# One buffer of exponentials instead of two, two group loads moved into segment 2, and eight groups corrected without VectorE

## The chip, the cores and the metric

The kernel runs on one core of a Trainium2 chip. Its engines work side by side: TensorE (PE) multiplies matrices, ScalarE (ACT) applies functions and copies, VectorE (DVE) does element-wise work, GpSimd (POOL) issues the gathers and scatters that take row numbers, and SyncE (SP) issues the plain transfers. Sixteen transfer engines, shared by all issuers, move the data between HBM and the on-chip memory. The metric is the device time of one execution in microseconds (us); the span of a profile is the time from the first to the last instruction of the program in one profiled execution.

## What is computed

The input is a table of 16384 rows of 256 floats and a segment number from 0 to 7 for each row. The numbers are not sorted. `searchsorted` over them gives a start for each segment, and a row takes part in its segment's attention if its distance from that start fits into a padded table of 3072 places (a negative distance counts from the end). Cut to what matters:

```python
q, k, v = feat @ Wq, feat @ Wk, feat @ Wv
starts = jnp.searchsorted(bids, jnp.arange(B))
pos = jnp.arange(N) - starts[bids]
qp, kp, vp = (zeros(B, LMAX, ...).at[bids, pos].set(x) for x in (q, k, v))
scores = where(mask, einsum('bld,bmd->blm', qp, kp), NEG)
rp = einsum('blm,bmd->bld', softmax(scores), vp)
t = rp[bids, pos] @ Wt
tn = (t - t.mean(0)) / sqrt(t.var(0) + EPS) * gamma + beta
return feat + relu(tn)
```

A row that lies outside its segment's table reads the row at the table's edge, so most of the 16384 results are `feat` plus one of at most sixteen edge rows, and only some 4700 rows have a result of their own.

## The kernel before

The function `fast_path` records all instructions of the five engines in one order, and a small recording layer (`Program.op`, L587, and `settle`, L625) works out from the memory that each reads and writes which semaphores it waits for. Nothing reorders an engine's instructions: the order of the calls is the order on each engine. A transfer issued by SyncE waits, and everything behind it on SyncE waits with it.

**The attention** runs over the eight segments (the loop at L1743, index `e`, and `u` for steps within a segment). A segment has up to six tiles of 128 rows. GpSimd gathers a segment's rows into `xs` two segments ahead (`list_half`, L1202, issued at step 0); one segment ahead they are transposed (`xt_main`, step 0), multiplied into queries and keys (`project`, L1252, steps 1 and 3) and values (`values`, L1272). `scores` (L1285) forms the products of keys and queries; ScalarE writes their exponentials, for the first four query tiles into `pa` and for the last two into `pb`. `attend` (L1318) multiplies the exponentials with the values, `attended` (L1328) divides and writes the result to `tk`, and SyncE stores it to the table `t_rows` in HBM, four tiles after step 3 and two after step 5. Of `q`, `k`, `vs` and `pa` there are two buffers each, which segments take in turn (`e % 2`). The exponentials of segment e+1 are made at steps 3 and 4 of segment e, after the `attend` calls for tiles 0 to 3.

**The statistics.** `acc` collects sums and squares of the results; the squares of the last tiles lie in `sq`, four slots behind `tk`. After segment 7 TensorE forms `sums` from them (L1888 to L1898), and a short chain on VectorE and ScalarE makes the scale, the shift and the table `y3` of corrected edge rows.

**The tail** (L1903 to L2038). The 16384 rows are cut into 16 groups of 1024 rows (1 MB). For each group a load `group_in` (L1723) brings `feat` into a buffer; a unit of two tiles is corrected by adding a product of the one-hot table `hot` with `y3`; the group is stored. There are four units in a group and two ways to correct one. In the first, VectorE adds the product, in PSUM, to the buffer (L2002). In the second, TensorE first multiplies the buffer with the identity into the same PSUM bank, adds the product there, and ScalarE copies the bank back (L1991, L1998). `by_act` (L1987) says which unit goes which way. Groups are worked in pairs (index `c`), and PSUM banks 0 to 5 are taken in turn.

There are `NF` = 12 buffers `f0` to `f11` for the 16 groups. Most of them lie over memory that the attention has finished with, so that a load waits until that memory is free. `free_at` (L983) lists their places: three rooms of their own (groups 0 to 2), the lists (group 3), the region from `q0` to `pa0` (4 and 5), that of `w4`, `wvt`, `xT` and `vs0` (6 and 7), that of `q1`, `k1` and `pa1` (8 and 9), and that of `sq`, `pb` and `vs1` (10 and 11). Groups 12 to 15 take the buffers of groups 0 to 3 after these are stored.

Between the pairs, VectorE normalises the attention's own rows (`rows`, L1968), and GpSimd writes them over the stored groups, 128 rows at a time (`put`, L892). It may only do so after every group that holds rows of that segment has been stored: SyncE waits for a store to land and adds one to the semaphore `done` (`finish`, L1978), and GpSimd waits for a count worked out from the segment numbers. With this input the counts are 3 for segment 0, 5 for segments 1 and 2, 7 for segments 3 to 5 and 11 for segments 6 and 7. At most two stores stand behind the one that SyncE waits for (L2011).

Of the kernel before, what the change touches and what calls it, by code (L numbers as in the profile page):

```python
# [9 lines left out]
F32 = mybir.dt.float32  # L10
# [4 lines left out]
AF = mybir.ActivationFunctionType  # L15
# [5 lines left out]
P = 128  # L21
NB = 8
# [6 lines left out]
FT = 6  # L29
# [873 lines left out]
def fast_path(nc, feat, bids, wq, wk, wv, wt, gamma, beta, out, bad):  # L903
# [5 lines left out]
    GT = 8  # L909
# [19 lines left out]
    def new(name, shape, dtype=F32):  # L929
        nonlocal end  # L930
        size = mybir.dt.size(dtype)
        for d in shape[1:]:
            size *= d
        plan.append((name, shape, dtype, end))
        h = at(name, shape, dtype, end)
        end += size + -size % 32
        return h
# [8 lines left out]
    def addr(h):  # L946
        return pg.where[h.name][1]
# [4 lines left out]
    def tiles_of(e):  # L952
        return FT if e else 4

    rooms = [new(f"room{i}", [P, GT, D]) for i in range(3)]
    xs = new("xs", [P, TS, D])
    hot = new("hot", [P, NG // 2, GT, P], F8)
    SQ = 4
    tk = new("tk", [P, TS + SQ, D])
    sq = [tk[:, TS + i, :] for i in range(SQ)]  # L960
    pa, vs, q, k = [None] * 2, [None] * 2, [None] * 2, [None] * 2
    at_end = addr(tk) + TS * D * 4
    pb = new("pb", [P, FT, QB])
    vs[1] = new("vs1", [P, FT, D + 1])
    at_scores = end
    q[1], k[1] = new("q1", [P, FT * P]), new("k1", [P, 2, P])
    pa[1] = new("pa1", [P, FT, QA])
    at_values = end
    junk = [new("junk0", [P, P]), new("junk1", [P, P])]
    w4, wvt = new("w4", [P, DH, P]), new("wvt", [P, DH, D])  # L970
    xT = new("xT", [P, DH, FT * P])
    vs[0] = new("vs0", [P, FT, D + 1])
    at_before = end
    q[0], k[0] = new("q0", [P, FT * P]), new("k0", [P, 2, P])
    pa[0] = new("pa0", [P, FT, QA])
    at_lists = end
    lm, dl = new("lm", [P, NL, J], BF16), new("dl", [P, 2, J + 2], BF16)
    ge = new("ge", [P, 2, FT * P], BF16)
# [2 lines left out]
    crow, cown, cidx = new("crow", [32, 1], I32), new("cown", [32, 1]), new("cidx", [32, 1], I32)  # L981
    cdiag = new("cdiag", [32, 2 * NB])
    free_at = [addr(x) for x in rooms] + [at_lists]  # L983
    for x in (at_before, at_values, at_scores, at_end):
        free_at += [x, x + 8192]
    NF = len(free_at)
    fb = [at(f"f{i}", [P, GT, D], F32, x) for i, x in enumerate(free_at)]

# [1 line left out]
    ones_n = new("ones_n", [P, P])  # L990
    acc = new("acc", [P, 2, D])
    by_reads = new("by_reads", [P, 3, P])
    ecat = new("ecat", [P, 2, D])
    xl, tl = new("xl", [P, LT, D]), new("tl", [P, LT, D])
    eb = [new("eb0", [P, GT * P], BF16), new("eb1", [P, GT * P], BF16)]
# [256 lines left out]
    def project(e, c):  # L1252

        b = nb()
        lo, n = c * QA, (QA if c == 0 else QB)
        for t in (None,) if c == 0 else (4, 5):
            at0, w = (0, QA) if t is None else ((t - 4) * P, P)
            with present(e, t or 0):
                for h in range(DH):
                    pg.mm(  # L1260
                        b[:, at0 : at0 + w], w4[:, h, :], xT[:, h, lo + at0 : lo + at0 + w],
                        start=(h == 0), stop=(h == DH - 1),
                    )
        qe, ke = q[e % 2], k[e % 2]
        with present(e, 4 * c):
            pg.act(qe[0:96, lo : lo + n], b[0:96, 0:n], AF.Identity, bias=cqk[0:96, :])
            pg.act(qe[96:P, lo : lo + n], b[0:32, 0:n], AF.Identity, bias=cqk[0:32, :])
            for t in range(n // P):
                g = 32 * t
                pg.copy("DVE", ke[g : g + 32, c, :], b[96:P, t * P : (t + 1) * P])  # L1270
# [12 lines left out]
            pg.copy("ACT", vs[e % 2][:, 2 * c : 2 * c + 2, 0:D], b[:].rearrange("p (t d) -> p t d", t=2))  # L1283

    def scores(e, c, tiles):  # L1285
        qe, ke = q[e % 2], k[e % 2]

        def bank_of(t, lo, w):
            at0 = lo + (QB if t >= 4 and c == 1 else 0)
            return ps_s[t % 4][:, at0 : at0 + w]  # L1290

        def product(t, lo, w):
            g = slice(32 * (t % 4), 32 * (t % 4) + 32)
            pg.mm(bank_of(t, lo, w), ke[g, t // 4, :], qe[g, c * QA + lo : c * QA + lo + w])

        if c == 0:
            for t in tiles:
                with present(e, t):
                    product(t, 0, QA)
            for t in tiles:  # L1300
                with present(e, t):
                    m = e * FT + t
                    pg.act(pa[e % 2][:, t, :], bank_of(t, 0, QA), AF.Exp, bias=mask[:, m : m + 1])
            return
        with pg.given(e, 0):
            for t in range(5):
                product(t, 0, P)
        with pg.given(e, 1):
            for t in range(5):
                product(t, P, P)  # L1310
            product(5, 0, QB)
        for k_, parts in ((0, [(t, 0, P) for t in range(5)]), (1, [(t, P, P) for t in range(5)] + [(5, 0, QB)])):
            with pg.given(e, k_):
                for t, lo, w in parts:
                    m = e * FT + t
                    pg.act(pb[:, t, lo : lo + w], bank_of(t, lo, w), AF.Exp, bias=mask[:, m : m + 1])

    def attend(e, u):  # L1318
        po = ps_o[u % 2]
        src, w = (pa[e % 2], u) if u < 4 else (pb, u - 4)  # L1320
        for t in (0, 1, 2, 4, 5, 3) if e else range(4):
            with present(e, max(t, u)):
                pg.mm(
                    po[:, 0 : D + 1], src[:, t, w * P : (w + 1) * P], vs[e % 2][:, t, :],
                    start=(t == 0), stop=(t == 3),
                )
# [396 lines left out]
    def group_in(i, after=()):  # L1723
        pg.dma("SP", fb[i % NF][:], feat3[ORDER[i]], after)

    def repeated(t):
        pg.act(rsq[:], tl[:, t, :], AF.Square)
        pg.tt(acc[:, 0, :], acc[:, 0, :], tl[:, t, :], ALU.add)
        pg.tt(acc[:, 1, :], acc[:, 1, :], rsq[:], ALU.add)

    lag, ready = [], []
    steps = {0: (1, 2, 3, 4, 5), 1: (0, 1, 3), 2: (1, 2, 3, 5)}
    def third_list():
# [9 lines left out]
    for e in range(NB - 1):  # L1743
# [10 lines left out]
        for u in range(FT):  # L1754
# [43 lines left out]
            if u == 0:  # L1798
                if ahead < NB:
                    second()  # L1800
                if e == NB - 2:
                    for t in range(LT):
                        pg.gather(tl[:, t, :], t_rows[0 : (NB - 2) * FW, :], ridl[:, t : t + 1], (NB - 2) * FW)
                    group_in(3)
                if e:
                    xt_main(n, 0)
                    xt_main(n, 1)
# [20 lines left out]
                    ready.append(lag.pop(0))  # L1828
            if e == 0 and u in (1, 5):
                pg.copy("ACT", spot[:], ones[:, 0:1])  # L1830
            if e == NB - 3 and u in (1, 2, 4):
                group_in(u // 2 if u > 1 else 0)
            if e == NB - 2 and u == 4:
                pg.gather(ecat[:, 0, :], t_rows[0:EDGE, :], eidx[:], EDGE)
                group_in(4)
                group_in(5)
            if e == NB - 2 and u >= 3:
                repeated(u - 3)
            if e == 4 and u == 3:
# [66 lines left out]
    units = 0  # L1906
    pg.set("POOL", y3[:], 0.0)
    group_in(10)
    for t in range(LT):
        pg.gather(tl[:, t, :], t_rows, ridl[:, t : t + 1], NB * FW)  # L1910

# [70 lines left out]
    for c in range(NG // 2):  # L1982
        for r in range(2):
            i = 2 * c + r
            for x in range(0, GT, 2):
                early = (i, x) in first_units
                by_act = x >= (2 if 4 <= c < 7 else 4) if c else x in (2, 4) and early  # L1987
                pf = bank[units % 6]
                units += 1
                if by_act and not early:  # L1990
                    pg.mm(pf[:], ident[:], unit(i, x), start=True, stop=False)  # L1991
                for u in range(2):
                    pg.mm(
                        pf[:, u * D : (u + 1) * D], hot[:, c, x + u, :], y3[:, r, :],
                        start=not (by_act or early), stop=True,
                    )
                if by_act:
                    pg.copy("ACT", unit(i, x), pf[:])  # L1998
                elif early:
                    pg.copy("DVE", unit(i, x), pf[:])  # L2000
                else:
                    pg.tt(unit(i, x), unit(i, x), pf[:], ALU.add)  # L2002
            f = fb[i % NF]
            stores.append(
                pg.op("SP", lambda e, i=i, f=f: e.dma_start(out3[ORDER[i]], f[:]), [f[:]], [], dma=True)
            )
            if i == 2:
                group_in(NF - 1)
            if i >= 4 and i - 4 + NF < NG:
                group_in(i - 4 + NF)  # L2010
            while counted < i - 1 or counted < min(i, 3):  # L2011
                finish(stores[counted])
                counted += 1
        for e in {1: (0,), 2: (1,), 3: (2,), 4: (3, 4), 5: (5, 6), 6: (7,)}.get(c, ()):
            rows(e)
        if c == 6:
            normal([(ExitStack, tl[:, a:b, :], xl[:, a:b, :], b - a) for a, b in ((0, 2), (2, LT))])
        if c == 7:
            pg.ts(good[:], rdens[:], LIM, ALU.is_lt)
            pg.stt(good[:], rdens[:], 1.0 / LIM, good[:], ALU.is_gt, ALU.mult, accum=odd[:])  # L2020
            pg.ts(odd[:], odd[:], -1.0, ALU.mult, float(TT), ALU.add)
            pg.red(cnt_f[:, 0:1], over[:])
# [78 lines left out]
```

## Time and profile before

| | us |
|---|---|
| median of 3 runs | 284.02 |
| the 3 runs | 282.41, 284.02, 286.15 |
| time of the profiled execution | 284.55 |
| its span | 282.2 |
| PE busy | 242.6 |
| DVE busy | 195.5 |
| ACT busy | 140.0 |
| POOL busy | 106.2 |

Busy times are of the whole span, in which the attention and the tail have different limits, so they are read together with the stretches that the prediction quotes. A row of the table of stretches names the stretch, its length, then for each engine its busy time and the number of its instructions, then the granted clock of TensorE, the share of the sixteen transfer engines that was busy, and what they moved in GB/s. In a row of the timeline stand the start, the duration, the engine (with a q where its sequencer issues a transfer), the line, the operation, what it writes `<-` what it reads, how many such instructions were merged, and in brackets the idle time before and what ended it. A merged row's duration runs from the first start to the last end. The line of most instructions is that of a helper (L808 is `mm`, L827 `tt`, L880 `dma`), so the tile names tell them apart; `f` is a group's buffer, `out<-f` its store, `out<-tk` a write of single rows.

### The profile page before, as it was taken

Reading aid. Unit: us, or ns where it says so; the run is one execution under the profiler, and the core shown is the slowest. Engines: PE = TensorE matmul, PEld = TensorE weight load, DVE = VectorE, ACT = ScalarE, POOL = GpSimd, SP = SyncE. Lnnn points to the kernel's source line nnn. Section 1 sums busy time; section 2 is a strip of 40 time slices with the busy share of each in tenths; the row PEclk is TensorE's granted clock in tenths of the full one; section 3 lists DMA queues with packets and bytes.
Section 4 is the critical chain, followed back from the end, with each engine's and each line's share of the span. In section 5 each row is a group of like instructions: output and inputs, shape, how many; then the busy total and the mean of one; then the engine's idle time right before and its main releaser. Section 6 shows DMA issues by size and latency. Waiting matters only on the chain.

```text
span 282.2 us, 4370 instructions
## 1 busy us (share of the span) xinstructions
PE 242.6 (86%) x1219; PEld 168.7 (60%) x1219; DVE 195.5 (69%) x631; ACT 140.0 (50%) x304; POOL 106.2 (38%) x141
## 2 busy tenths in 40 slices
PE   1789979999999999999999999989998898195540
PEld 0656757667778777877787787667554444042210
DVE  8766887768878553465438618955499999999920
ACT  6246553792794764666546644586233344032210
POOL 4517174407104500256317001210030527577774
PEclk9999999999999999999999999999999999779975
DMA  3202799523122330221238485199989999999994
GB/s 101 58 7 77 243 336 363 177 90 97 30 74 85 110 103 8 95 82 54 89 85 251 147 263 180 35 345 394 352 340 361 378 415 412 404 408 388 396 368 171
DMA packets 24643, 59.06 MB, mean 209 GB/s; under 512 B 4355, under 2 KB 17005, under 8 KB 20517
## 3 DMA queue, kind: packets, MB, share of 16 engines
q1 hardware_dynamic: 19013, 47.74, 46.6%
q0 software_dynamic: 4784, 10.17, 10.8%
q10 hardware_dynamic: 816, 0.79, 0.8%
q8 instruction: 14, 0.23, 0.3%
q14 instruction: 16, 0.13, 0.1%
HBM read 26.93 MB, written 28.54 MB: 197 GB/s over the span
## 4 chain that ended last, share of the span: by engine, by line
PE 63%; DVE 21%; ACT 5%; issue 5%; POOL 2%; DVEq 1%; POOLq 0%; ACTq 0%
PE ps L808 60%; DVE ps L827 4%; PE ps L813 3%; DVE f L827 3%; DVE tk L827 3%; DVE tk L849 2%; POOL out L895 2%; ACT tk L818 2%; ACT pa L818 2%; DVE k L824 1%; DVEq L773 1%; ACT vs L823 1%; DVE sel L838 1%; DVE acc L827 0%; DVE w L827 0%
## 5 line engine op out<-in xcount | busy, mean ns | idle before, releaser
L885 POOL DMA_INDIRECT xs<-in_r_feat,idx x46 | 47.2, 1026 | 90.5 <-DVE idx L827 48.8
L808 PE MATMUL ps<-vs,pa 128*128 128x257 f32 x312 | 74.4, 386 | 1.8 <-ACT tk L818 1.5
L808 PEld LDWEIGHTS ps<-vs,pa 128*128 128x128 f32 x312 | 57.0, 190 | 12.7 <-ACT tk L818 2.8
L808 PE MATMUL ps<-f,ident 128*128 128x512 f32 x80 | 44.1, 645 | 15.8 <-DVE f L827 15.8
L895 POOL DMA_INDIRECT out<-tk,idx x39 | 38.4, 985 | 25.9 <-DVE tk L827 8.6
L823 ACT COPY f<-ps 128x512 f32<-128x512 f32 x37 | 21.5, 586 | 46.0 <-PE ps L808 46.0
L818 ACT ACTIVATE tk<-ps,rdens 128x256 f32<-128x256 f32 x48 | 22.6, 481 | 40.8 <-DVE rdens L862 40.6
L1363 DVE SCALAR_TENSOR_TENSOR acc<-tk,reads_r,acc 128x512 f32<-128x512 f32 x43 | 32.2, 748 | 9.9 <-ACT tk L818 9.3
L808 PE MATMUL ps<-wvt,xT 128*128 128x256 f32 x156 | 36.5, 383 | 0.0
L808 PEld LDWEIGHTS ps<-wvt,xT 128*128 128x128 f32 x156 | 29.1, 190 | 8.0 <-issue 2.8
L818 ACT ACTIVATE pa<-ps,mask 128x512 f32<-128x512 f32 x39 | 23.9, 689 | 7.8 <-PE ps L808 7.8
L808 PEld LDWEIGHTS ps<-y,hot 128*128 128x128 fp8e4 x128 | 12.7, 100 | 23.9 <-issue 21.8
L808 PEld LDWEIGHTS ps<-f,ident 128*128 128x128 f32 x80 | 13.3, 202 | 20.6 <-DVE f L827 11.5
L862 DVE RECIPROCAL rdens<-ps 128x1 f32<-128x1 f32 x44 | 7.4, 168 | 21.9 <-PE ps L808 21.7
L808 PE MATMUL ps<-y,hot 128*128 128x256 bf16 x128 | 20.4, 278 | 0.4 <-DVE y L827 0.4
L824 DVE COPY k<-ps 32x128 f32<-32x128 f32 x40 | 11.8, 294 | 11.7 <-PE ps L808 11.0
L808 PE MATMUL ps<-xT,w 128*128 128x512 f32 (+1 forms) x60 | 19.3, 453 | 0.5 <-ACT xT L818 0.3
L808 PE MATMUL ps<-vs,pb 128*128 128x257 f32 x82 | 19.6, 387 | 0.0
L808 PE MATMUL ps<-q,k 32*128 32x512 f32 (+2 forms) x154 | 18.9, 478 | 0.0
L808 PEld LDWEIGHTS ps<-vs,pb 128*128 128x128 f32 x82 | 15.1, 189 | 5.7 <-issue 2.3
L885 POOL DMA_INDIRECT tl<-t_rows,places x6 | 6.0, 999 | 31.5 <-DMA t_rows<-tk 20.2
L834 DVE TENSOR_SCALAR_CACHE_REDUCE junk<-ps,rcol 128x128 f32<-128x128 f32 x49 | 14.6, 346 | 4.4 <-PE ps L808 4.4
(259 smaller groups left out, 330.1 us busy)
## 6 DMA issues: line engine op xcount, KB each, us to landing
f<-in_r_feat SPq DMA_DIRECT2D x16, 1024.0 KB, 10.2
out<-f SPq DMA_DIRECT2D x16, 1024.0 KB, 10.1
xs<-zt SPq DMA_DIRECT2D x6, 768.0 KB, 7.4
t_rows<-tk SPq DMA_DIRECT2D x8, 512.0 KB, 3.3
eb<-edge_of SPq DMA_DIRECT2D x16, 128.0 KB, 3.2
t_rows<-tk SPq DMA_DIRECT2D x6, 256.0 KB, 2.4
xs<-in_r_feat,idx POOLq DMA_INDIRECT x46, 3.0
out<-tk,idx POOLq DMA_INDIRECT x39, 6.2
```

What stands on the lines that cost most here:

```text
L808: "PE", lambda e: e.matmul(out, lhsT, rhs, start=start, stop=stop, skip_group_check=True),
L813: return self.op("PE", lambda e: e.transpose(out, in_, ident), [in_, ident], [out])
L818: "ACT", lambda e: e.activation(out, in_, func, bias=bias, scale=scale), [in_, *more], [out]
L823: return self.op("ACT", lambda e: e.copy(out, in_), [in_], [out])
L824: return self.op(eng, lambda e: e.tensor_copy(out, in_), [in_], [out])
L827: return self.op(eng, lambda e: e.tensor_tensor(out, a, b, op), [a, b], [out])
L834: lambda e: e.tensor_scalar(out, a, s1, s2, op0, op1, accum_out=accum, **({"saturate": False} if out.dtype == F8 else {}))
L849: else e.scalar_tensor_tensor(out, a, s, b, op0, op1),
L862: return self.op("DVE", lambda e: e.reciprocal(out, in_), [in_], [out])
L885: lambda e: e.indirect_dma_start(out=out, out_offset=None, in_=table, in_offset=bass.IndirectOffsetOnAxis(ap=ind, axis=0), bounds_check=n ...
L895: lambda e: e.indirect_dma_start(out=table, out_offset=bass.IndirectOffsetOnAxis(ap=ind, axis=0), in_=src, in_offset=None, bounds_check=n ...
L1363: lambda e: e.scalar_tensor_tensor(acc[:], two, one, acc[:], ALU.mult, ALU.add),
```

## The change

The second buffers of `q` and `pa` go, and their room is given to two more rooms for groups, so that there are still twelve buffers. `k0` moves into the region of `w4`, and the two junk tiles of the list search (which are written and never read) into the room of `by_reads`, which is filled only in segment 7. The loads of groups 0 and 1 are issued in segment 2, at steps 2 and 4, those of groups 2 to 4 in segment 5 at the places where groups 0 to 2 were, that of group 5 where that of group 3 was. The places of groups 10 and 11 are swapped, and group 11's load goes out behind that of group 10. `finish` is called for stores 0 to 2 only when store 3 has been issued. Of the last eight groups all units go by TensorE and ScalarE.

```diff
-    rooms = [new(f"room{i}", [P, GT, D]) for i in range(3)]
+    rooms = [new(f"room{i}", [P, GT, D]) for i in range(5)]
...
-    q[1], k[1] = new("q1", [P, FT * P]), new("k1", [P, 2, P])
-    pa[1] = new("pa1", [P, FT, QA])
+    q, k[1] = new("q", [P, FT * P]), new("k1", [P, 2, P])
+    pa = new("pa", [P, FT, QA])
     at_values = end
-    junk = [new("junk0", [P, P]), new("junk1", [P, P])]
+    k[0] = new("k0", [P, 2, P])
...
-    at_before = end
-    q[0], k[0] = new("q0", [P, FT * P]), new("k0", [P, 2, P])
-    pa[0] = new("pa0", [P, FT, QA])
...
-    for x in (at_before, at_values, at_scores, at_end):
+    for x in (at_values, at_scores):
         free_at += [x, x + 8192]
+    free_at += [at_end + 8192, at_end]
...
+    junk = [at(f"junk{i}", [P, P], F32, addr(by_reads) + i * P * 4) for i in range(2)]
...
-                    pg.act(pa[e % 2][:, t, :], bank_of(t, 0, QA), AF.Exp, bias=mask[:, m : m + 1])
+                    pg.act(pa[:, t, :], bank_of(t, 0, QA), AF.Exp, bias=mask[:, m : m + 1])
...
+    EARLY = ((2, 2), (2, 4), (NB - 3, 1), (NB - 3, 2), (NB - 3, 4))
...
-                    group_in(3)
+                    group_in(5)
...
-            if e == NB - 3 and u in (1, 2, 4):
-                group_in(u // 2 if u > 1 else 0)
+            if (e, u) in EARLY:
+                group_in(EARLY.index((e, u)))
             if e == NB - 2 and u == 4:
                 pg.gather(ecat[:, 0, :], t_rows[0:EDGE, :], eidx[:], EDGE)
-                group_in(4)
-                group_in(5)
...
     group_in(10)
+    group_in(11)
...
-                by_act = x >= (2 if 4 <= c < 7 else 4) if c else x in (2, 4) and early
+                by_act = x >= (0 if c >= 4 else 4) if c else x in (2, 4) and early
...
-            if i == 2:
-                group_in(NF - 1)
             if i >= 4 and i - 4 + NF < NG:
                 group_in(i - 4 + NF)
-            while counted < i - 1 or counted < min(i, 3):
+            while i > 2 and counted < max(3, i - 1):
```

How SyncE's queue stands in segment 2, before (`tk` is the attention's result, `row_i` the table of row numbers, `at_h` that of the edge rows; a number behind a name is the program's):

```order
L880 DMA t_rows<-tk_54 128x2x256
L880 DMA t_rows<-tk_54 128x4x256
L880 DMA row_of<-row_i_182 128x128
L880 DMA t_rows<-tk_54 128x2x256
L880 DMA edge_of<-at_h_178 128x128
```

The same place after:

```order
L880 DMA t_rows<-tk_56 128x2x256
L880 DMA f0_78<-in_r_feat 128x2048
L880 DMA t_rows<-tk_56 128x4x256
L880 DMA f1_79<-in_r_feat 128x2048
L880 DMA row_of<-row_i_182 128x128
L880 DMA t_rows<-tk_56 128x2x256
L880 DMA edge_of<-at_h_178 128x128
```

The loads of groups 0 and 1 now stand ahead of the stores of segment 2's rows and of the table of row numbers. SyncE's queue from segment 6 to the first stores, before:

```order
L880 DMA f5_85<-in_r_feat 128x2048
L880 DMA f6_86<-in_r_feat 128x2048
L880 DMA f7_87<-in_r_feat 128x2048
L880 DMA t_rows<-tk_54 128x4x256
L880 DMA f8_88<-in_r_feat 128x2048
L880 DMA f9_89<-in_r_feat 128x2048
L880 DMA t_rows<-tk_54 128x2x256
L880 DMA f10_90<-in_r_feat 128x2048
L2005 DMA out_0<-f0_80 128x2048
L2005 DMA out_0<-f1_81 128x2048
L2005 DMA out_0<-f2_82 128x2048
L880 DMA f11_91<-in_r_feat 128x2048
```

And after:

```order
L880 DMA t_rows<-tk_56 128x4x256
L880 DMA f6_84<-in_r_feat 128x2048
L880 DMA f7_85<-in_r_feat 128x2048
L880 DMA t_rows<-tk_56 128x4x256
L880 DMA f8_86<-in_r_feat 128x2048
L880 DMA f9_87<-in_r_feat 128x2048
L880 DMA t_rows<-tk_56 128x2x256
L880 DMA f10_88<-in_r_feat 128x2048
L880 DMA f11_89<-in_r_feat 128x2048
L2004 DMA out_0<-f0_78 128x2048
L2004 DMA out_0<-f1_79 128x2048
L2004 DMA out_0<-f2_80 128x2048
```

The load of group 6 now follows segment 6's store of its first four tiles directly, and the load of group 11 has moved from behind the third store to ahead of the first. On TensorE, where group 8 begins (`ident` is the identity, `hot` the one-hot table, `ps` a PSUM bank), before:

```order
L808 MATMUL ps2<-y3_108,hot_53 128x256 x2
L808 MATMUL ps3<-f8_88,ident_92 128x512
L808 MATMUL ps3<-y3_108,hot_53 128x256 x2
L808 MATMUL ps4<-f8_88,ident_92 128x512
L808 MATMUL ps4<-y3_108,hot_53 128x256 x2
```

And after:

```order
L808 MATMUL ps2<-f8_86,ident_90 128x512
L808 MATMUL ps2<-y3_108,hot_55 128x256 x2
L808 MATMUL ps3<-f8_86,ident_90 128x512
L808 MATMUL ps3<-y3_108,hot_55 128x256 x2
L808 MATMUL ps4<-f8_86,ident_90 128x512
L808 MATMUL ps4<-y3_108,hot_55 128x256 x2
```

The first unit of group 8, which VectorE added to its buffer before, now has a product with the identity as well.

More of the change, by code (lines that the diff above doesn't have):

```diff
@@ L960, in fast_path @@
     sq = [tk[:, TS + i, :] for i in range(SQ)]
-    pa, vs, q, k = [None] * 2, [None] * 2, [None] * 2, [None] * 2
+    vs, k = [None] * 2, [None] * 2
     at_end = addr(tk) + TS * D * 4
@@ L1263, in project @@
                     )
-        qe, ke = q[e % 2], k[e % 2]
+        qe, ke = q, k[e % 2]
         with present(e, 4 * c):
@@ L1285, in scores @@
     def scores(e, c, tiles):
-        qe, ke = q[e % 2], k[e % 2]
+        qe, ke = q, k[e % 2]
         def bank_of(t, lo, w):
@@ L1319, in attend @@
         po = ps_o[u % 2]
-        src, w = (pa[e % 2], u) if u < 4 else (pb, u - 4)
+        src, w = (pa, u) if u < 4 else (pb, u - 4)
         for t in (0, 1, 2, 4, 5, 3) if e else range(4):
```

## The prediction

> **What bounds the kernel now.** I read the page first, for where the span's two halves part.
>
> ```profile
> span 282.2 us, 4370 instructions
> PEclk9999999999999999999999999999999999779975
> DMA  3202799523122330221238485199989999999994
> xs<-in_r_feat,idx POOLq DMA_INDIRECT x46, 3.0
> ```
>
> A slice is 282.2 / 40 = 7.06 us. Up to slice 26 (183 us) the transfer engines are mostly idle, the attention is computed, and there is room for transfers. From slice 26 to the last but one they stand at 8 or 9: this is the tail, in which groups are loaded, corrected, stored, and single rows written over them. The second view is the table of stretches, read for the share of the 16 transfer engines and their GB/s (the last two columns), to find out whether a 9 is full.
>
> ```profile
> 183.30:208.00 24.70, 22.66 (x93) 15.18 (x93) 14.63 (x41) 12.77 (x30) 1.52 (x2) 1.00 0.96 365
> 207.00:208.00 1.00, 1.00 (x12) 0.88 (x10) 1.00 (x2) 0.90 (x2) 0.00 (x0) 1.00 0.74 310
> 208.00:209.00 1.00, 0.91 (x8) 0.45 (x6) 0.97 (x3) 0.66 (x2) 0.25 (x1) 1.00 0.06 25
> 209.00:210.00 1.00, 1.00 (x4) 0.42 (x5) 1.00 (x2) 0.00 (x0) 0.77 (x1) 1.00 0.94 393
> 211.00:213.00 2.00, 2.00 (x12) 1.23 (x11) 1.65 (x4) 0.66 (x2) 1.06 (x2) 1.00 0.89 299
> 212.00:276.00 64.00, 43.58 (x166) 20.55 (x164) 55.33 (x108) 18.73 (x32) 38.07 (x40) 0.91 1.00 393
> ```
>
> From 212 to 276 us the share is 1.00 at 393 GB/s, so the tail is bound by bytes. Ahead of it there are holes only around the first store: 0.26 + 0.94 + 0.06 in 207 to 210, and 2 x 0.11 in 211 to 213, together 1.5 us.
>
> Third, SyncE's queue, on which all loads and stores of groups are issued in one order, and its waits:
>
> ```profile
> 182.88 0.38 SPq L880 DMA_DIRECT2D t_rows<-tk  x1
> 183.30 5.18 SPq L880 DMA_DIRECT2D f<-in_r_feat  x4
> 187.60 0.87 SPq L880 DMA_DIRECT2D f<-in_r_feat  x2
> 196.14 0.38 SPq L880 DMA_DIRECT2D t_rows<-tk  x1
> 199.19 0.42 SPq L880 DMA_DIRECT2D f<-in_r_feat  x1
> 208.27 4.91 SPq L2005 DMA_DIRECT2D out<-f  x3
> 213.23 1.15 SPq L880 DMA_DIRECT2D f<-in_r_feat  x1
> 236.50 35.73 SPq L2005 DMA_DIRECT2D out<-f  x8
> SPq L1979 <- DMA out<-f: 53.6, 16, 6.9
> SPq L2005 <- DVE f L827: 1.4, 1, 1.4
> L1979 SPq EVENT_SEMAPHORE  x16: 17/17/17, 212.7 to 280.6; - x16
> ```
>
> Of the four loads from 183.30 on, two (groups 4 and 5) go out at once and two (6 and 7) at 187.60. L1979 counts a store when it has landed: the first at 212.7, 4.4 us after its issue, the last at 280.6. SyncE waited 53.6 us for landings and 1.4 us for data. Fourth, GpSimd, which writes single rows over the stored groups and may do so only when enough stores have been counted:
>
> ```profile
> 220.32 1.02 POOL L895 DMA_INDIRECT out<-tk,idx  x1 [7.95 <-DVE tk L827]
> 230.29 0.98 POOL L895 DMA_INDIRECT out<-tk,idx  x1 [5.07 <-SPq L1979]
> 243.52 0.98 POOL L895 DMA_INDIRECT out<-tk,idx  x1 [1.93 <-SPq L1979]
> 278.31 0.98 POOL L895 DMA_INDIRECT out<-tl,idx  x1 [0.30 <-issue]
> ```
>
> From 243.52 on it issues 28 writes without a pause, (278.31 - 243.52) / 27 = 1.29 us each, and that run begins when store 6 has been counted. Both ends, the last store and the last row, hang on how soon the transfer engines get through the queue.
>
> **The change part by part.** *One buffer of exponentials and queries.* The next segment's exponentials overwrite those that the present segment reads. Each Exp waits for its score product anyway, and TensorE issues that product behind the last read of the old exponentials; for the queries the order is the same. I take 0. The cover is TensorE's order; without it the wait would be one segment's reads. The moved k and junk buffers are written by VectorE and read by engines as before: 0.
>
> *Two loads put into segment 2.* Two groups, 2 x 1.049 = 2.10 MB, leave the stretch after 183.30: 2.10 / 0.393 = 5.3 us of a full queue. They go out behind the two t_rows stores that SyncE issues at 62.33 and, the last of them, up to 62.33 + 16.10 = 78.43, where there is room:
>
> ```profile
> 62.00:70.00 8.00, 7.86 (x47) 5.63 (x46) 6.49 (x32) 3.37 (x8) 4.68 (x5) 1.00 0.27 86
> 62.33 16.10 SPq L880 DMA_DIRECT2D t_rows<-tk  x2
> 64.10 0.99 POOL L885 DMA_INDIRECT xs<-in_r_feat,idx  x1 [10.79 <-DVE idx L827]
> xs<-in_r_feat,idx POOLq DMA_INDIRECT x6, 5.8
> ```
>
> The first load meets the six gathers from 64.10 on. The page gives a median landing of 3.0 us for all 46, and the last six, from 140 us on and beside a group load, took 5.8. So the price lies between 0 and 2.8 us. I take 0: the gathered rows are transposed a whole segment later. The table row_of, stored soon after the second load, may be as late; 2.8 us stays in the range.
>
> *What the queue does without them.* Load 6 still waits until 187.60, for segment 6's value products. The first store's issue at 208.27 and the share of 0.06 up to 209 show 0.8 us from issue to bytes. So: t_rows (0.52 MB) ends at 182.88 + 0.8 + 1.3 = 185.0, and load 6 begins at 188.4: a hole of 3.4 us. Loads 6 and 7, 0.26 MB of t_rows and a gather of 0.13 MB, 2.49 MB in all, take 6.3 us to 194.7; the next t_rows is issued at 196.14 and begins at 196.9: a hole of 2.2 us. Together 5.6 us that are not idle now.
>
> *Group 11's load ahead of the first store* (now at 213.23, behind three stores). Its region, the squares, is free after the moment products, so it follows load 10 (199.19) by about 1 us. From 196.9 the queue holds 0.52 + 0.26 + 4 x 1.049 = 4.98 MB: to 209.6 at 393 GB/s, to 210.5 at the 365 of that stretch. That is 0.5 to 1.4 us later than store 0 begins now (209.06), but the 1.5 us of holes around that place are filled; SyncE no longer waits for store 0 before it issues store 2, which was part of them.
>
> Sum: 5.3 + 1.5 - 5.6 = 1.2 us gained. Counted from the first store on: load 11 is no longer behind it (2.7 us) and the hole at 211 to 213 is filled (0.2), against a start 0.5 to 1.4 us later, so 1.5 to 2.4 us. I take 1.7, between the two ways. The ends are 6.8 us gained, with no holes (5.3 + 1.5), and 1.6 lost, with 1.2 gained and the 2.8 of late gathers paid.
>
> The Trainium skill (DMA: Bandwidth & Descriptors, section Specifications) puts HBM's limit for one core at about 358 GB/s. By it the two loads would be worth 5.9 us and the gain 0.6 us more. The trace disagrees, with 393 GB/s over 64 us, so it is not used.
>
> *Groups 8 to 15 by TensorE and ScalarE alone.* Ten additions leave VectorE, ten TensorE products with the identity and ten ScalarE copies come in.
>
> ```profile
> 266.30 2.47 DVE L827 TENSOR_TENSOR f<-f,ps 128x512 f32<-128x512 f32 x4
> 226.63 1.02 PE L808 MATMUL ps<-f,ident 128*128 128x512 f32 x2
> 227.71 1.02 PE L808 MATMUL ps<-f,ident 128*128 128x512 f32 x2
> 246.04 2.08 PE L808 MATMUL ps<-f,ident 128*128 128x512 f32 x2 [6.86 <-DVE f L827]
> 248.33 1.91 PE L808 MATMUL ps<-f,ident 128*128 128x512 f32 x2
> 250.56 1.02 PE L808 MATMUL ps<-f,ident 128*128 128x512 f32 x2
> 244.00:248.00 4.00, 1.96 (x3) 0.74 (x4) 3.93 (x8) 0.00 (x0) 3.08 (x4) 0.50 1.03 399
> L823 ACT COPY f<-ps 128x512 f32<-128x512 f32 x37 | 21.5, 586 | 46.0 <-PE ps L808 46.0
> ```
>
> VectorE loses 10 x 0.62 = 6.2 us (four took 2.47), and TensorE no longer stands still for 6.86 us behind it. A unit on TensorE is two passes of 1.02 us and two short products, 227.71 - 226.63 = 1.08 us from start to start, so 32 units from 226.63 on end at 261.2, long before store 15's issue at 271.9. ScalarE's 0.59 us a unit lies beside that. On the path it is worth 0: the wait for data was 1.4 us, while older stores were still in the queue. If those were gone it would be worth 1.4.
>
> **The sum.** The profiled execution took 284.55 us, 2.35 more than its span; 1.7 less is 282.85. It stands 0.53 above the median of the runs, 284.02, so I forecast 284.02 - 1.7 = 282.3 us. The last counted store would come at 278.9 and the last row at 276.6.
>
> **The rivals.** *The whole two loads come off.* If load 6 went out by 185 and the queue never ran dry, 6.8 us would go: 277.2. The row at 187.60 speaks against it, since the buffer is set free by TensorE, whose work isn't moved.
>
> *Nothing is left of it.* The holes are 1.7 us wider than I make them, which leaves 284.0, or a gather in segment 2 is late and on TensorE's path, 284.02 - 1.2 + 2.8 = 285.6; between them 284.8. For it speaks that the sum is a difference of two figures of 5 us; against it that the holes around the first store are sure to be filled.
>
> *TensorE's clock makes the last groups late* (the other side). All eight last groups now hang on TensorE. The row at 244 to 248 shows the granted clock at 0.50 after 6.86 us without work, and there a unit took 248.33 - 246.04 = 2.29 us. If half clock held for all 32 units, store 15 would be ready at 226.63 + 32 x 2.29 = 299.9 and land 4.4 later, at 304.3 instead of 280.6: 307.7 us. It decides from the point where store 15 is issued after 280.6 - 4.4 = 276.2, that is 1.55 us a unit, or half clock for 39% of the units; a loss over 2% needs 1.73 us, 54%. Against it: the clock fell only where TensorE had stood still, waiting for VectorE, and that wait goes.
> The Trainium skill (TensorE: Matmul & The Clock Gate, Part 1: The HAM clock gate) says that an idle window of about 3.4 us halves the clock and a busy one restores it; the trace agrees at this place (6.86 us idle, then 0.50), and by that rule the steady stream of units would keep the clock up.
>
> **How the numbers follow.** Chances: my forecast (1 to 3 us gained) 0.60; nothing left 0.28; both loads off 0.07; the clock 0.05. The range takes in the forecast and most of the second: from 284.02 - 4.6 = 279.4, two thirds of the way to the first rival, to 285.6, the end with late gathers. About 2% (5.7 us) is what a measurement of this kernel can tell from no change, its runs lying between 282.41 and 286.15. Faster by more needs the first rival: 0.07. Slower by more needs the clock: 0.05. Within 2%: 0.88.
>
> **What would show it.** Loads at about 63 and 79 us; a stretch of nearly no transfers around 186 to 188 and another near 195 to 197; none from 207 to 213; GpSimd's long run beginning near 241.8; no wait of ScalarE's Exp for a read of the old exponentials; TensorE at full clock from 227 to 261. I am wrong if the last store is counted before 276 or after 280.6, if the holes are absent, or if TensorE's chain up to 200 us has moved.

## The result and the profile after

The changed kernel took 281.15 us, the median of 6 runs (281.00 to 282.67); the kernel before took 284.32 in 6 runs (282.41 to 286.15). The ratio is 0.9897, 95% interval 0.9852 to 0.9942: a gain of 2.9 us, between 1.6 and 4.2. That is within the 2% band; the 1.7 us of the forecast lie just inside the interval, and its time of 282.3 stands 1.15 above the median. The profiled execution took 281.0 us. Some executions of a kernel are slower as a whole than the others, and the ratios, here and below, leave them out, so that a ratio can differ from that of two medians.

The page of the changed kernel, with the lines that answer to those shown of before (a slice is 278.6 / 40 = 6.97 us):

```profile
span 278.6 us, 4403 instructions
PEclk9999999999999999999999999999999999999955
DMA  3102799627162321230517573429799999999995
xs<-in_r_feat,idx POOLq DMA_INDIRECT x46, 3.0
```

The transfer engines now show a 2 in slice 26 (181 to 188 us) and a 7 in slice 28 (195 to 202), where before the 9s of the tail began at 183: the opening of the tail is no longer full. From slice 29 on it is, as before. The clock stays at 9 up to the last two slices; before, it fell to 7 in two slices around 247 us, and again near the end.

The table of stretches of the changed kernel (columns as in the prediction; last three: granted clock, share of the transfer engines, GB/s):

```profile
183.05:208.00 24.95, 22.91 (x95) 15.22 (x95) 14.89 (x42) 13.01 (x31) 2.38 (x3) 1.00 0.79 280
186.00:188.00 2.00, 1.22 (x5) 0.77 (x5) 1.75 (x6) 1.71 (x5) 1.34 (x1) 1.00 0.00 0
195.00:197.00 2.00, 2.00 (x12) 1.75 (x11) 0.90 (x4) 1.57 (x6) 0.00 (x0) 1.00 0.25 82
207.00:208.00 1.00, 1.00 (x11) 0.71 (x10) 1.00 (x3) 1.00 (x3) 0.51 (x1) 1.00 1.01 426
208.00:209.00 1.00, 0.91 (x6) 0.57 (x6) 0.97 (x2) 0.41 (x1) 0.69 (x2) 1.00 1.03 434
211.00:213.00 2.00, 2.00 (x11) 1.10 (x10) 1.65 (x4) 0.91 (x2) 0.10 (x1) 1.00 1.04 430
227.00:261.00 34.00, 33.84 (x127) 15.52 (x125) 31.97 (x63) 18.27 (x32) 24.43 (x26) 1.00 1.01 417
```

Two holes have opened, at 186 to 188 (nothing moved at all) and at 195 to 197; the whole stretch up to 208 moves 280 GB/s where it moved 365, with 0.21 x 24.95 = 5.2 us of its time without transfers (0.04 x 24.70 = 1.0 before). The holes around the first store are gone: 208 to 209 moves 434 GB/s where it moved 25, and 211 to 213 has 430 in place of 299. From 227 to 261 TensorE is busy for 33.84 of 34 us at full clock.

SyncE's timeline, its counts of landed stores, and GpSimd's timeline:

```profile
62.06 0.36 SPq L880 DMA_DIRECT2D t_rows<-tk  x1
62.47 0.47 SPq L880 DMA_DIRECT2D f<-in_r_feat  x1
77.81 0.36 SPq L880 DMA_DIRECT2D t_rows<-tk  x1
78.21 0.51 SPq L880 DMA_DIRECT2D f<-in_r_feat  x1
...
182.61 0.38 SPq L880 DMA_DIRECT2D t_rows<-tk  x1
187.33 0.80 SPq L880 DMA_DIRECT2D f<-in_r_feat  x2
195.88 0.38 SPq L880 DMA_DIRECT2D t_rows<-tk  x1
196.30 1.50 SPq L880 DMA_DIRECT2D f<-in_r_feat  x2
197.89 0.40 SPq L880 DMA_DIRECT2D t_rows<-tk  x1
198.35 1.36 SPq L880 DMA_DIRECT2D f<-in_r_feat  x2
208.00 12.65 SPq L2004 DMA_DIRECT2D out<-f  x5
```

```profile
L1978 SPq EVENT_SEMAPHORE  x16: 17/17/17, 214.7 to 277.0; - x16
```

```profile
236.89 0.98 POOL L895 DMA_INDIRECT out<-tk,idx  x1 [0.30 <-DVE ps L827]
240.12 0.98 POOL L895 DMA_INDIRECT out<-tk,idx  x1 [2.25 <-SPq L1978]
274.92 0.98 POOL L895 DMA_INDIRECT out<-tl,idx  x1 [0.30 <-issue]
```

The first loads go out at 62.47 and 78.21. Loads 6 and 7 still wait until 187.33, and the last two loads (groups 10 and 11) go out together at 198.35. Up to 208.00 the program stands only 0.27 us earlier than before (first store at 208.27). The last store is counted at 277.0 in place of 280.6, and GpSimd's long run goes from 240.12 to 274.92 in place of 243.52 to 278.31, with the same 1.29 us from write to write. So all of the gain but 0.27 us arises behind the first store's issue: from there to the last count it took 280.6 - 208.27 = 72.3 us, and now 277.0 - 208.0 = 69.0.

In that stretch the transfer engines move about the same bytes in less time, 72.23 x 0.376 = 27.2 MB before and 69.00 x 0.392 = 27.0 MB now. Group 11's load stands ahead of it now only in the order of the queue: issued at 199.31, it lands 12.0 us later, at 211.3, and is still under way when the first store is issued. The whole stretch, its first 12 us and the 8 us behind them, before:

```profile
208.27:280.50 72.23, 47.22 (x183) 22.49 (x182) 58.67 (x113) 20.29 (x35) 43.39 (x44) 0.88 0.95 376
208.27:220.27 12.00, 11.20 (x53) 5.84 (x53) 11.51 (x19) 4.67 (x9) 3.00 (x3) 1.00 0.95 350
220.27:228.27 8.00, 6.91 (x31) 3.42 (x29) 7.71 (x15) 3.05 (x6) 3.99 (x4) 1.00 0.97 391
```

And after:

```profile
208.00:277.00 69.00, 51.54 (x203) 24.62 (x202) 52.80 (x103) 26.16 (x45) 42.88 (x44) 0.90 0.98 392
208.00:220.00 12.00, 11.20 (x53) 5.86 (x53) 11.51 (x19) 4.67 (x9) 2.49 (x3) 1.00 1.01 423
220.00:228.00 8.00, 6.91 (x29) 3.24 (x27) 7.71 (x15) 3.28 (x6) 5.11 (x6) 1.00 0.95 313
```

In the 12 us TensorE, VectorE and ScalarE do the same work, and the transfer engines move 423 GB/s and not 350, which is 73 x 12 = 0.88 MB more. In the 8 us behind them it is the other way round: 313 GB/s and not 391, 78 x 8 = 0.62 MB less. Over the 20 us some 0.25 MB are left of the lead, 0.6 us at 393 GB/s.

### The profile page after: what moved, and what is told of

The parts are those of the page before. It is cut to its first block, busy times and chain, and to the rows that moved or that the text cites. A ratio compares the mean times of both kernels' runs of the same rounds, so it can differ in the third digit from the quotient of the medians.

```text
span 278.6 us, 4403 instructions
## 1 busy us (share of the span) xinstructions
PE 246.8 (89%) x1239; PEld 170.4 (61%) x1239; DVE 189.6 (68%) x621; ACT 145.8 (52%) x314; POOL 106.6 (38%) x141
## 3 DMA queue, kind: packets, MB, share of 16 engines
q0 software_dynamic: 4784, 10.17, 10.9%
## 4 chain that ended last, share of the span: by engine, by line
PE 64%; DVE 19%; issue 6%; ACT 6%; POOL 3%; DVEq 1%; POOLq 0%; ACTq 0%
PE ps L808 60%; DVE ps L827 4%; PE ps L813 3%; DVE tk L827 3%; POOL out L895 2%; DVE tk L849 2%; ACT tk L818 2%; ACT pa L818 2%; DVE f L827 1%; DVE k L824 1%; ACT vs L823 1%; DVEq L773 1%; DVE sel L838 1%; DVE acc L827 0%; DVE w L827 0%
## 5 line engine op out<-in xcount | busy, mean ns | idle before, releaser
L808 PE MATMUL ps<-f,ident 128*128 128x512 f32 x100 | 50.6, 596 | 1.9 <-DVE f L827 1.8
L823 ACT COPY f<-ps 128x512 f32<-128x512 f32 x47 | 27.3, 586 | 30.1 <-PE ps L808 30.1
L808 PE MATMUL ps<-y,hot 128*128 128x256 bf16 x128 | 21.4, 273 | 0.4 <-DVE y L827 0.4
L808 PEld LDWEIGHTS ps<-f,ident 128*128 128x128 f32 x100 | 15.6, 191 | 5.5 <-issue 5.0
L823 ACT COPY vs<-ps 128x512 f32<-128x512 f32 x20 | 11.8, 592 | 10.8 <-PE ps L808 10.8
```

The lines of the kernel that those rows point to most:

```text
L808: "PE", lambda e: e.matmul(out, lhsT, rhs, start=start, stop=stop, skip_group_check=True),
L823: return self.op("ACT", lambda e: e.copy(out, in_), [in_], [out])
```

## The experiments

Three theories. A: what counts is how many loads are through before the first store and how steadily the queue runs from there; the early loads leave holes and are worth nothing. B: each load that leaves the stretch after 183 us is worth its bytes, 2.7 us. C: VectorE's relief by the units that moved to ScalarE makes the gain. Besides times, two places are read from each profile: the count of store 6, from the issue of segment 6's store of four tiles (59.7 us before, 56.5 after), and the 12 us from the first store's issue, as above. The 12 us show whether the queue is full there; what that is worth they do not show, since most of it can be lost again in the next 8.

The first four kernels ran on a chip on which the kernel before took 298.97 us (median of 29 runs, 296.72 to 303.39), so that only ratios to it on that chip are used.

**Early loads back in their old places** (the changed kernel, edited):

```diff
-    EARLY = ((2, 2), (2, 4), (NB - 3, 1), (NB - 3, 2), (NB - 3, 4))
+    EARLY = ((NB - 3, 1), (NB - 3, 2), (NB - 3, 4))
...
-                    group_in(5)
+                    group_in(3)
...
+                group_in(4)
+                group_in(5)
```

> The changed kernel with no load in segment 2: groups 0 to 2 are loaded in segment 5, group 3 in segment 6 at step 0, groups 4 and 5 at step 4 of segment 6, as before; buffers, group 11's load and the rest stay as changed. Theory A (what counts is how many loads are through before the first store; the loads moved to segment 2 only leave holes of 5.6 us in which they would have run for nothing): as fast as the changed kernel or up to 1 us slower, 281.2 to 282.2 us, ratio to before 0.989 to 0.993. Theory B (each load taken out of the stretch after 183 us is worth its 2.7 us): nearly all of the gain goes, 283.5 to 284.5 us, ratio 0.997 to 1.001. Theory C (VectorE's relief carries the gain): 281.2 us, ratio 0.989.

298.09 us, but its 6 runs went from 291.63 to 304.29 and gave no ratio. In its profile store 6 is counted at 57.1, 0.6 us later than in the changed kernel. That fits A, but profiles of single executions differ by more than this (see the short version); since the times decided nothing, the kernel was run again (below).

**Only group 11's load moved** (the kernel before, edited; the regions of groups 10 and 11 are swapped as in the change):

```diff
-    for x in (at_before, at_values, at_scores, at_end):
+    for x in (at_before, at_values, at_scores):
         free_at += [x, x + 8192]
+    free_at += [at_end + 8192, at_end]
...
     group_in(10)
+    group_in(11)
...
-            if i == 2:
-                group_in(NF - 1)
```

> The kernel before with one part of the change alone: the places of groups 10 and 11 are swapped and group 11 is loaded right behind group 10, ahead of the first store. Two buffers of exponentials, loads, counts and units as before. Theory A: 2 to 3 us gained, 281.3 to 282.3 us, ratio 0.989 to 0.993. Theory B: nothing or little, since the same number of bytes stands behind 183 us, 283.5 to 284.3 us, ratio 0.997 to 1.0. Theory C: 284.3 us, ratio 1.0.

299.49 us, ratio 0.9924 (0.9872 to 0.9975); the ratio rests on half of its 12 runs. Store 6 is counted at 58.0. With the old counts store 2 waits behind the count of store 0 until 32.4 (30.0 before). This one edit carries most of the gain, as A expected (0.989 to 0.993).

**Only the units of groups 8 to 15 moved to ScalarE** (the kernel before, edited):

```diff
-                by_act = x >= (2 if 4 <= c < 7 else 4) if c else x in (2, 4) and early
+                by_act = x >= (0 if c >= 4 else 4) if c else x in (2, 4) and early
```

> The kernel before with one part of the change alone: all units of groups 8 to 15 by TensorE and ScalarE. Theories A and B: no change, 283.8 to 284.6 us, ratio 0.998 to 1.001. Theory C: about 3 us gained, 281.2 us, ratio 0.989.

301.09 us, ratio 1.0068 (1.0034 to 1.0102): alone, on this chip, it was slightly slower, which A and B did not expect either (0.998 to 1.001). C falls.

**The changed kernel with VectorE's units back** (the same line the other way round):

> The changed kernel with one part undone: of groups 8 to 15 VectorE again adds one unit in four (two in four in the last pair). Theories A and B: as the changed kernel, at most 1.4 us slower if store 14 now waits for VectorE while the queue behind it is shorter, 281.2 to 282.5 us, ratio 0.989 to 0.994. Theory C: 284.3 us, ratio 1.0.

296.04 us, ratio 0.9889 (0.9843 to 0.9935): without the moved units the gain is all there. C falls a second time.

The next four kernels ran on a chip on which the kernel before took 284.43 us (283.2 to 286.7, 34 runs); each is an edit of the changed kernel.

**Counts as before:**

```diff
-            while i > 2 and counted < max(3, i - 1):
+            while counted < i - 1 or counted < min(i, 3):
```

> The changed kernel with one part undone: SyncE again waits for store 0 to land before it issues store 2, and for store 1 before store 3. Read from the issue of segment 6's store of four tiles to the count of store 6 (59.7 us before, 56.5 in the changed kernel). Theory A: store 0 now stands behind group 11's load, so that SyncE waits for it about 2 us longer than before and store 2 goes out late; the transfer engines run dry for 0.5 to 1 us, the count comes at 57 to 57.5, the time is 0.5 to 1 us above the changed kernel's. Theory B: no difference, 56.5.

282.42 us, ratio 0.9914 (0.9873 to 0.9956). Store 2 goes out 31.4 us after segment 6's store (29.1 in the changed kernel), store 6 is counted at 57.3. Against the changed kernel's 0.9897 this is at most a small loss, which the intervals do not separate from none.

**Group 11's load behind the third store again:**

```diff
     group_in(10)
-    group_in(11)
...
+            if i == 2:
+                group_in(NF - 1)
```

> The changed kernel with one part undone: group 11 is loaded behind store 2 again. Theory A: the holes from about 24 to 31 us after segment 6's store come back, larger than before, since the queue ahead of them ends earlier; the count of store 6 comes at 59 to 60, and nearly all of the gain is gone, ratio to before 0.997 to 1.0. Theory B: two loads fewer stand behind that point, the count comes near 57 and the gain stays, ratio 0.989 to 0.992.

284.61 us, ratio 1.002 (0.9986 to 1.0054). The whole gain is gone, with the early loads, the single buffer, the swapped places of groups 10 and 11, the later counts and ScalarE's units all in place. Store 6 is counted at 58.8, a little before A's 59 to 60 and well behind B's 57. The 12 us from its first store's issue:

```profile
211.16:223.16 12.00, 11.21 (x53) 5.86 (x53) 11.51 (x19) 4.67 (x9) 2.73 (x3) 1.00 0.96 335
```

335 GB/s, near the 350 of the kernel before.

**One load more, in the first hole** (the load of group 2 is issued a second time, where load 4 stood; the same data arrive twice, so 1.05 MB are added):

```diff
             if e == NB - 2 and u == 4:
                 pg.gather(ecat[:, 0, :], t_rows[0:EDGE, :], eidx[:], EDGE)
+                group_in(2)
```

> The changed kernel with one transfer more: group 2, which is in its buffer already, is loaded a second time at step 4 of segment 6, where groups 4 and 5 were loaded before. The result is the same. Theory A: the hole ahead of load 6 is 3.4 us long and takes a load of 2.7 us for nothing: count of store 6 at 56.5 to 57, time within 0.3 us of the changed kernel. Theory B: each load is worth 2.7 us wherever it stands after 183 us: count at 59.2, time 2.7 us above the changed kernel's.

281.29 us, ratio 0.9891 (0.9855 to 0.9927); store 6 is counted at 55.7, even before A's 56.5 to 57, where B expected 59.2. A load at that place is free. Its stretch that is the hole in the changed kernel (0.00 and 0 GB/s there):

```profile
186.00:188.00 2.00, 1.01 (x5) 0.68 (x4) 1.64 (x4) 1.78 (x6) 0.70 (x1) 1.00 0.97 332
```

So moving that load away earns nothing either, and B falls.

**One load more, ahead of the first store** (the load of group 9 a second time, behind that of group 11):

```diff
     group_in(11)
+    group_in(9)
```

> The changed kernel with one transfer more: group 9 is loaded a second time behind group 11's load, ahead of the first store. The result is the same. Theories A and B both: there is no hole left there, so the load costs its full 2.5 to 2.7 us: count of store 6 at 59.0 to 59.3, time 2.5 to 2.7 us above the changed kernel's. If it costs less than 1 us, the transfer engines are not what bounds the tail, and both fall.

283.82 us, ratio 0.9987 (0.9945 to 1.0029); store 6 is counted at 58.9. Against the changed kernel it costs (0.9987 - 0.9897) x 284.4 = 2.6 us, with intervals of about 1.2 us to each side of both ratios; its bytes are worth 1.049 / 0.393 = 2.7 us. Ahead of the first store one load more is not free.

The last three ran on a chip on which the kernel before took 283.84 us (282.29 to 286.66, 23 runs).

**The short version** (the kernel before with the edit that moves group 11's load, shown above, and the later counts):

```diff
-            while counted < i - 1 or counted < min(i, 3):
+            while i > 2 and counted < max(3, i - 1):
```

> The kernel before, with two parts of the change: group 11's load is issued ahead of the first store (the regions of groups 10 and 11 swapped), and stores 0 to 2 are counted only when store 3 has been issued. Two buffers of exponentials and queries stay, no load moves into segment 2, VectorE's units stay. Theory A (only what stands ahead of the first store and does not stall SyncE's queue counts; early loads leave holes): within 0.8 us of the changed kernel, ratio 0.988 to 0.993 against the kernel before; store 6 counted 56.5 to 57.3 us after the issue of segment 6's store of four tiles. Theory B (each load out of the stretch after 183 us is worth 2.7 us): two loads are missing there, so 3 us or more slower than the changed kernel, ratio 1.0 or above.

281.97 us, ratio 0.9898 (0.9857 to 0.9939), the changed kernel's own ratio (the two medians alone give 0.9934). The profiled execution was one of the longer ones (283.9 us); store 6 is counted in it at 58.6, beyond the 56.5 to 57.3 of theory A and 2.1 us behind the changed kernel's, so that this place, in one profile, does not tell such kernels apart. The 12 us from the first store's issue:

```profile
208.24:220.24 12.00, 11.20 (x53) 5.85 (x53) 11.51 (x19) 4.67 (x9) 3.01 (x3) 1.00 1.01 424
```

The 8 us behind them move 308 GB/s, as slow a stretch as the changed kernel's 313.

**Early loads back in their old places, once more:**

> The changed kernel with the loads of groups 0 and 1 back in segment 5 and those of groups 4 and 5 back in segment 6, as before: the price of the early loads in runs that spread less than the first time. Theory A: at most 0.8 us slower than the changed kernel, ratio 0.988 to 0.994; store 6 counted 56.5 to 57.3 us after segment 6's store of four tiles. Theory B: 5 us slower than the changed kernel, ratio about 1.008.

281.96 us, ratio 0.9917 (0.9882 to 0.9952), within theory A and far from B's 1.008. Its profile was taken in its longest execution, of 286.42 us, so that its count of store 6 (58.6) says little. The early loads are worth nothing that these runs can tell (0.9917 against 0.9897, 0.6 us, with intervals of 1 us and more to each side).

**Only the later counts** (the kernel before with the one line of counts):

> The kernel before with one edit: stores 0 to 2 are counted only when store 3 has been issued, so that SyncE does not stand at store 0 or 1 with later stores behind it; group 11's load stays behind the third store's issue. Theory A: the counts alone are worth at most 0.8 us, since the holes ahead of the first store stay; ratio 0.996 to 1.001. Rival: the counts alone are most of the gain, ratio 0.990 or below, store 6 counted 57.5 us or less after segment 6's store of four tiles.

284.4 us, ratio 1.0009 (0.9969 to 1.0049): alone they are worth nothing that can be told, and the rival of 0.990 falls. The count of store 6 is at 58.4, no later than in the profile of the short version. The first holes are still there, and the 12 us from the first store's issue are those of the kernel before:

```profile
208.00:209.00 1.00, 0.91 (x8) 0.45 (x6) 0.97 (x3) 0.63 (x2) 0.00 (x0) 1.00 0.16 66
208.24:220.24 12.00, 11.21 (x53) 5.85 (x53) 11.51 (x19) 4.67 (x9) 3.01 (x3) 1.00 0.93 350
```

The 8 us behind them move 400 GB/s, where the short version has 308.

All that have a ratio, sorted by where group 11's load stands (the first column of GB/s is that of the 12 us from the first store's issue, the last that of the 8 us behind them):

| kernel | group 11's load | ratio (95% interval) | GB/s | next 8 us |
|---|---|---|---|---|
| changed | ahead | 0.9897 (0.9852 to 0.9942) | 423 | 313 |
| VectorE's units back | ahead | 0.9889 (0.9843 to 0.9935) | 424 | 323 |
| load added in the hole | ahead | 0.9891 (0.9855 to 0.9927) | 425 | 334 |
| short version | ahead | 0.9898 (0.9857 to 0.9939) | 424 | 308 |
| counts as before | ahead | 0.9914 (0.9873 to 0.9956) | 425 | 345 |
| late loads, second time | ahead | 0.9917 (0.9882 to 0.9952) | 424 | 284 |
| only group 11's load | ahead | 0.9924 (0.9872 to 0.9975) | 410 | 324 |
| load added ahead of store 0 | ahead, and one more | 0.9987 (0.9945 to 1.0029) | 423 | 350 |
| only later counts | behind | 1.0009 (0.9969 to 1.0049) | 350 | 400 |
| group 11's load late again | behind | 1.002 (0.9986 to 1.0054) | 335 | 400 |
| only ScalarE's units | behind | 1.0068 (1.0034 to 1.0102) | 347 | 400 |

No ratio below that of the changed kernel stands apart from it; the short version equals it with two of its parts. Both columns of GB/s follow the place of the load and not the time: the kernel with one load more ahead has 423, then 350, and no gain, and in every kernel with the load ahead the 8 us are slower than the 391 of the kernel before. Store 6 is counted at 55.7 to 58.6 in the profiles with the load ahead, at 58.9 with one more, and at 58.4 to 59.7 with the load behind.

## Why the prediction was right, and where it was off

- *The tail is bound by the transfer engines' bytes.* Right as far as one load at each of two places shows: ahead of the first store it costs 2.6 us, in a hole nothing.
- *The two loads in segment 2 and the holes cancel (5.3 against 5.6 us).* Right. The holes came where they were put, at 186 to 188 and at 195 to 197, since load 6 still waits (187.33) and the next store to `t_rows` still goes out at 195.88. The stretch up to 208 has 5.2 - 1.0 = 4.2 us more without transfers, a little under the 5.6, and moves 2.0 MB less (24.95 x 0.280 against 24.70 x 0.365), the two loads' 2.10, so that the first store finds as many bytes left as before. Putting those loads back changed the time by nothing that can be told, and filling the first hole with another load cost nothing.
- *No price for late gathers in segment 2.* Right: the gathers' median landing is still 3.0 us, and the first store is issued 0.27 us earlier, not later.
- *One buffer of exponentials and queries costs 0.* Right as far as the changed kernel shows: ScalarE's waits ahead of the exponentials add up to 7.8 us, all for TensorE, on the page of either kernel, and the first store is not issued later. The row cannot tell a wait for the score product from one for the last read of the old exponentials, both being TensorE's. The part was not run alone.

```profile
L818 ACT ACTIVATE pa<-ps,mask 128x512 f32<-128x512 f32 x39 | 23.9, 689 | 7.8 <-PE ps L808 7.8
```

- *Group 11's load ahead of the first store is the gain.* Right in kind: with it alone the ratio was 0.9924, and taking it back took all. **The size is less sure.** The forecast counted the load's bytes (2.7 us) and the hole at 211 to 213 (0.2), against a start of the stores 0.5 to 1.4 us later, and took 1.7 us; measured are 2.9 (1.6 to 4.2), so that the runs hardly tell the two apart, and 3.55 in the two profiles (284.55 and 281.0 us). The later start came as forecast: the last load ahead of the stores landed at 210.1 before (issued at 199.19, 10.9 us to landing) and at 211.3 now, 1.2 us later, and store 0 was counted at 214.7 in place of 212.7. That store 0 was issued 0.27 us earlier is no gain by itself, with that load still under way.

What the forecast left out is the rate once the queue is full. It priced what stands behind the first store at 393 GB/s and the holes; these bytes, about as many as before, went at 376 before and at 392 now. Of the 0.88 MB by which the first 12 us lead, worth 0.88 / 0.393 = 2.2 us, the holes are 12 x (1.01 - 0.95) = 0.7 us, and the other 1.5 us come from packets that took longer: with a share of about 1.00, at two places a few microseconds apart, the kernel before moved 417 and 320 GB/s.

```profile
213.00:215.00 2.00, 2.00 (x10) 0.99 (x9) 1.97 (x4) 1.10 (x2) 0.00 (x0) 1.00 1.01 417
217.00:221.00 4.00, 3.34 (x14) 1.78 (x15) 3.95 (x8) 1.31 (x3) 0.68 (x1) 1.00 1.00 320
```

So a share of 1.00 is not "the full rate". But these 1.5 us were not gained: the changed kernel has 399 GB/s at 217 to 221 and its own slow stretch right behind, 305 GB/s at 220.2 to 225.7, and after 20 us only about the worth of the holes is left. The rest of the difference lies later, in the next 40 us (402 GB/s at 228.27 to 268.27 before, 415 at 228 to 268 after) and at the end. The traces do not tie it to the load: in the 40 us that begin 20 us behind the first store's issue, the kernel with only the later counts (load behind) moved 409 GB/s and the short version (load ahead) 412, in executions of 283.12 and 283.9 us. So behind the first store's issue the traces place some 0.6 us, the worth of the holes, at the seam; why the runs show more, and why packets are slow at some places, stays open.

- *Groups 8 to 15 without VectorE are worth 0.* Right: with VectorE's units back the ratio was 0.9889, against 0.9897. TensorE's part was right to the figure: units at 226.15 and 227.23, 1.08 us apart, without idle time between them.

```profile
226.15 1.02 PE L808 MATMUL ps<-f,ident 128*128 128x512 f32 x2
227.23 1.02 PE L808 MATMUL ps<-f,ident 128*128 128x512 f32 x2
...
244.00:248.00 4.00, 4.00 (x17) 1.89 (x15) 3.83 (x10) 2.03 (x5) 3.08 (x4) 1.00 1.01 412
```

At 244 to 248, where the clock was 0.50 behind 6.86 us without work, it is 1.00 now. The rule of the Trainium skill (TensorE: Matmul & The Clock Gate, Part 1: The HAM clock gate), that busy windows keep the clock up, agrees with it, and the rival of a halved clock didn't come.

- *Its ends.* Forecast were a long run from 241.8, a last row at 276.6 and a last count at 278.9; they came at 240.12, 274.92 and 277.0, each 1.7 to 1.9 us earlier, by which the profiles' difference exceeds the forecast. The rival in which nothing is left needed wider holes at 186 to 197 or late gathers; neither came. The rival in which both loads come off needed load 6 to go out by 185; it went at 187.33.
- *The limit of 358 GB/s* that the Trainium skill (DMA: Bandwidth & Descriptors, section Specifications) gives for one core, as half of the 716 of a stack that two cores share, was set aside for the trace's 393. Rows of 417 GB/s over 34 us (227 to 261) and 423 over 12 us are above it again; this program runs on one core.

## What to carry to other kernels

Where one queue feeds a byte-bound tail, the first place to look is the seam between the last loads and the first stores. Here a load that went out ahead of the first store gained 2.9 us with the rest of the change, and a second one beside it cost as much as its bytes. Moving bytes out of the tail earns nothing if a buffer that comes free late leaves a hole in their place; first find which later transfer would fill it. Read a stretch by its share and by its GB/s, since full transfer engines moved up to a quarter less here, and read it far enough: what 12 us had gained, the next 8 mostly gave back.

## What the runs showed of the hardware

- Transfer engines with a share of 1.00 to 1.03 moved 320 GB/s at one place (217 to 221, before) and 434 at another (208 to 209, after).
- A slow stretch moves with the load: in the 8 us that begin 12 us behind the first store's issue, the eight kernels of the table with group 11's load ahead moved 284 to 350 GB/s, the three with it behind 400 each and the kernel before 391. The cause was not tried.
- On the chip on which the kernel before took 298.97 us, the tail has stops that the profiles from other chips do not show. In the changed kernel with VectorE's units back, from 268 to 272 us TensorE worked for 1.39 us, GpSimd for 1.16 and the other two hardly at all, and the transfer engines stood nearly still:

```profile
268.00:272.00 4.00, 1.39 (x5) 0.45 (x3) 0.00 (x0) 0.03 (x1) 1.16 (x2) 0.85 0.20 71
```

The waits of that kernel name as the end of VectorE's wait something that the profile matches to no instruction of the core ("remote"), once for 7.1 us:

```profile
DVE f L827 <- remote: 7.1, 1, 7.1
```

What that is was not tried. The holes and rates around the first store are those of the other chips (347 GB/s with group 11's load behind the third store, 410 to 424 with it ahead), and the two kernels with the load ahead that have a ratio are faster there too.
